# Giving out the last layer's result as one sequence of 32 blocks, with the next batch's messages between them

## The chip, the cores and the metric

The kernel runs on one core of one Trainium2 chip. The metric is device time in microseconds (us) of one execution; lower is better. A core has five engines that run side by side, each through its own instructions in order: TensorE (PE in the profile, its weight loads PEld), VectorE (DVE), ScalarE (ACT), GpSimd (POOL) and SyncE (SP), which here issues nearly all DMAs.

## The reference

Four layers work on `x` of shape 4 x 128 x 128 x 128 (batch, two spatial axes, channels), each as `x = x + layer(groupnorm(x))`: a deformable convolution, a scan of 1-D convolutions over rows, a message layer, and a triangle layer. The change touches only the code of the last two:

```
def _L2_conv_ref(inputs, Wself, Wm, Wk):
    message_m = sum(inputs, axis=2); message_k = sum(inputs, axis=1)
    return inputs @ Wself.T + (message_m @ Wm.T)[:, :, None, :] + (message_k @ Wk.T)[:, None, :, :]

def _L3_conv_ref(x, ...):
    xn = layer_norm(x, norm_g, norm_b)
    left  = (xn @ left_w  + left_b)  * sigmoid(xn @ lgate_w + lgate_b)
    right = (xn @ right_w + right_b) * sigmoid(xn @ rgate_w + rgate_b)
    out_gate = sigmoid(xn @ ogate_w + ogate_b)
    out = einsum('bkjd,bkid->bijd', left, right)
    out = layer_norm(out, onorm_g, onorm_b) * out_gate
    return out @ to_out_w + to_out_b
```

The group norm ahead of each layer has 32 groups of 4 channels. All data are 32-bit floats.

## The kernel before, in words

`tile_preact_convs` calls `deform_layer` (layer 0), `scan_layer` (layer 1) and `message_and_triangle` (layers 2 and 3) one after the other. The last one starts near 4116 us; it is the subject here. It goes through the four batches `b`. `X` (in on-chip memory, 128 x 128 x 128) holds a batch's x3, the input of the triangle layer; `L` (same size) the left factor, later the triangle's result; `R_0` and `R_1` hold a quarter of the right factor each, and between batches quarters of the input `x2T`. In DRAM lie `x3d` (x3, for the residual) and `gates` (the output gates). Sizes: a group is `JG` = 32 columns, a block `JB` = 4 columns, so a batch has 4 groups of 8 blocks; the projections are cut into `NQ` = 4 quarters of 32 hidden channels and go in blocks of `QB` = 8 columns.

For a batch, the stages are lists of closures that each emit a few instructions on several engines:

- `sums_of(b)`: `prelude` (group-norm factors and message vectors), 32 `rows` items (L1321 one matmul of 512 columns, L1327 four DVE operations that add the messages and write X, L1332 one ACT square that sums), and `close`, which stores all of X to `x3d` by four DMAs of 2 MB (L1343) and makes the scale `s3` and shift `t3` of layer 3's group norm. `fetch` (L1311) loads a quarter of `x2T` (2 MB) into `R`; two quarters are fetched near the last triangle, the other two from within `rows`.
- `turned(b, g)`: for each block of group g, scale X in place (ACT, L1398), transpose on PE (L1406), copy back (ACT, L1407), statistics on DVE (L1409); `close` computes the layer norm's factors (L1370 to L1381, with one square root on ACT).
- `spread(b, g)`: normalize (DVE, L1426), transpose back (L1435, L1436), gate matmul and sigmoid (L1441, L1445), and store the gate (L1446).
- `projected(b, q, ...)`: for quarter q, 16 blocks over the whole batch, each of 8 matmuls (16 in the profile, L1466), one sigmoid (ACT, L1470) and two products (DVE, L1472, into `L` and `R[q % 2]`).
- `triangle(b, q)`: 8 blocks of matmuls of R with L (L1484) and an ACT copy into L (L1488).
- `counted_out(b, g)`: DVE statistics of L (L1499) and the factors.
- `given(b, g)`: a software pipeline over the 8 blocks of group g. Step k loads the gate of block k+1 (L1514) and the x3 columns of block k (L1520), normalizes block k (ACT L1529, DVE L1534), turns block k-1 (PE transpose L1544, ACT L1546, POOL product with the gate L1547), and puts block k-2 (PE L1555 and L1559 add residual and output projection, DVE L1564 or ACT L1562 copies to `res`, SP stores it, L1565). So each group has 10 steps, of which the last two only drain.

The order on every engine, SP's DMA queue included, is the order in which closures run (`manual_schedule`). `weave` interleaves lists evenly by their lengths:

```
n = min((i for i in range(len(parts)) if done[i] < len(parts[i])),
        key=lambda i: (2 * done[i] + 1) / len(parts[i]))
```

A batch then goes: `turned(b, 0)` alone; for g = 0 to 4 a weave of `turned(b, g + 1)`, `spread(b, g)` and the quarter-0 projection of group g - 1 (the norm stage); for q = 1 to 3 a weave of `projected(b, q)` over the whole batch with `triangle(b, q - 1)`; `triangle(b, 3)`; then `counted_out(b, 0)` woven with the first half of `sums_of(b + 1)`; then the four `given(b, g)`, each woven with `counted_out(b, g + 1)`, the first also with the second half of `sums_of(b + 1)`.

Buffers that matter: `work` (two, shared by the square's output, the sigmoid and the product with the gate), `res` (two), gate and `x3cols` (three each), and three pools of two PSUM buffers: `ps_q` for message sums and projections, `ps_t` for transposes and triangle, `ps_g` for gates, output and small sums.

Of the kernel before, what the change touches and what calls it, by code (L numbers as in the profile page):

```python
# [9 lines left out]
F32 = mybir.dt.float32  # L10
I32 = mybir.dt.int32
BF16 = mybir.dt.bfloat16
AF = mybir.ActivationFunctionType
# [43 lines left out]
def make_consts(nc, pool):  # L57

    c = Consts()
    c.ident = pool.tile([P, P], F32, name="ident")  # L60
    make_identity(nc, c.ident)
    c.ones = pool.tile([P, P], F32, name="ones")
    nc.vector.memset(c.ones, 1.0)
    c.mean = pool.tile([P, P], F32, name="mean")
    nc.vector.memset(c.mean, 1.0 / P)

    c.center = pool.tile([P, P], F32, name="center")
    nc.vector.tensor_scalar(c.center, c.ident, -1.0 / P, None, ALU.add)

    c.gmean = pool.tile([P, P], F32, name="gmean")  # L70
    nc.vector.memset(c.gmean, 1.0 / GS)
    gview = c.gmean.rearrange("p (g r) -> p g r", r=GS)
    nc.gpsimd.affine_select(
        out=gview, in_=gview, pattern=[[-GS, NGN], [0, GS]], compare_op=ALU.is_ge,
        fill=0.0, base=0, channel_multiplier=1,
    )
    nc.gpsimd.affine_select(
        out=gview, in_=gview, pattern=[[GS, NGN], [0, GS]], compare_op=ALU.is_ge,
        fill=0.0, base=GS - 1, channel_multiplier=-1,
    )  # L80
    c.eps = pool.tile([P, 1], F32, name="eps")
    nc.vector.memset(c.eps, GN_EPS)
    return c
# [1094 lines left out]
def message_and_triangle(tc, c, x2T, x3d, gates, counted, w2, w3, out):  # L1178
# [10 lines left out]
    JB = 4  # L1189
    QB = 8  # L1190
    QC = 4 * DQ
    NW = NQ * QC
    with ExitStack() as ctx:
        wp = ctx.enter_context(tc.tile_pool(name="l3w", bufs=1))
# [80 lines left out]
        def prelude(b):  # L1275
# [6 lines left out]
            msg = one.tile([P, 2, S], F32, name="msg")  # L1282
            nc.vector.tensor_scalar(msg[:, 0], sum_w[:, b], s2, tsum, ALU.mult, ALU.add)
            nc.vector.tensor_scalar(msg[:, 1], sum_h[:, b], s2, tsum, ALU.mult, ALU.add)
            twide = one.tile([P, S], F32, name="twide")
            nc.vector.tensor_scalar(twide, c.ones, t2, None, ALU.mult)
            pm = small_ps([P, 2, S], "msg_ps")
            nc.tensor.matmul(pm[:, 0], lhsT=wm, rhs=msg[:, 0], start=True, stop=False)
# [24 lines left out]
        def sums_of(b):  # L1313

            todo = [lambda: prelude(b)]

            def rows(y0):
                ws, z, less, lessb, squares = got[b]
                at = y0 % DQ
                pz = ps_q.tile([P, JB, S], F32, name="self_ps", tag="ps_q")  # L1320
                nc.tensor.matmul(  # L1321
                    pz, lhsT=ws, rhs=R[y0 // DQ % 2][:, at : at + JB, :], start=True, stop=True
                )
                if at + JB == DQ and y0 + DQ < S:
                    fetch(b, y0 // DQ + 2)
                for i in range(JB):
                    nc.vector.scalar_tensor_tensor(  # L1327
                        X[:, :, y0 + i], pz[:, i], z[:, 0, y0 + i : y0 + i + 1], z[:, 1],
                        ALU.add, ALU.add,
                    )  # L1330
                junk = two.tile([P, S, JB], F32, name="work", tag="work")
                nc.scalar.activation(  # L1332
                    junk, X[:, :, y0 : y0 + JB], AF.Square, bias=lessb,
                    accum_out=squares[:, y0 // JB : y0 // JB + 1],
                )

            todo += [lambda y0=y0: rows(y0) for y0 in range(0, S, JB)]

            def close():
                _, _, less, lessb, squares = got[b]  # L1340
                for g in range(NG_J):
                    js = slice(g * JG, (g + 1) * JG)
                    nc.sync.dma_start(x3d[b, :, js, :], X[:, js, :])  # L1343
                e = one.tile([P, 1], F32, name="e3")
                nc.vector.tensor_reduce(e, squares, AX.X, ALU.add)
                pg = small_ps([P, 1], "mean_ps")
                nc.tensor.matmul(pg, lhsT=c.gmean, rhs=less, start=True, stop=True)
                lg = one.tile([P, 1], F32, name="lg3")
                nc.vector.tensor_copy(lg, pg)
                d = one.tile([P, 1], F32, name="d3")  # L1350
                nc.vector.tensor_tensor(d, less, lg, ALU.subtract)
                nc.vector.tensor_tensor(d, d, d, ALU.mult)
                nc.vector.scalar_tensor_tensor(d, e, 1.0 / (S * S), d, ALU.mult, ALU.add)
                pv = small_ps([P, 1], "var_ps")
                nc.tensor.matmul(pv, lhsT=c.gmean, rhs=d, start=True, stop=True)
                var = one.tile([P, 1], F32, name="var3")
                nc.vector.tensor_copy(var, pv)
                s3 = two.tile([P, 1], F32, name="s3")
                nc.scalar.activation(s3, var, AF.Sqrt, bias=c.eps)
                nc.vector.reciprocal(s3, s3)  # L1360
                t3 = two.tile([P, 1], F32, name="t3")
                nc.vector.scalar_tensor_tensor(t3, lg, outb, s3, ALU.subtract, ALU.mult)
                got[b] = (s3, t3)

            return todo + [close]

        def factors(stats, name):

# [21 lines left out]
        def turned(b, g):  # L1390
# [8 lines left out]

            def block(k):  # L1400
                j0 = g * JG + k * JB
                if (k + 1) * JB < JG:
                    scale(k + 1)
                pt = ps_t.tile([P, JB, S], F32, name="turn_ps", tag="ps_t")
# [98 lines left out]

            return [lambda k=k: block(k) for k in range(JG // JB)] + [close]

        def given(b, g):

            n = JG // JB
            pend = {}

            def load(k):
                j0 = g * JG + k * JB
                gt = three.tile([P, JB, S], F32, name="gate", tag="load")
                nc.sync.dma_start(gt, gates[b, :, j0 : j0 + JB, :])  # L1514
                pend[k] = (gt,)

            def load_x3(k):
                j0 = g * JG + k * JB
                xr = three.tile([P, JB, S], F32, name="x3cols")
                nc.sync.dma_start(xr, x3d[b, :, j0 : j0 + JB, :])  # L1520
                pend[k] += (xr,)

            def norm(k):
                mu, r, off = known["o", b, g]
                cen = normed[k % 2]
                for j in range(JB):
                    i = k * JB + j
                    if j % 2:
                        nc.scalar.activation(  # L1529
                            cen[:, j], L[:, :, g * JG + i], AF.Identity,  # L1530
                            bias=off[:, i : i + 1], scale=r[:, i : i + 1],
                        )
                    else:
                        nc.vector.tensor_scalar(  # L1534
                            cen[:, j], L[:, :, g * JG + i], mu[:, i : i + 1], r[:, i : i + 1],
                            ALU.subtract, ALU.mult,
                        )
                pend[k] += (cen,)
# [9 lines left out]
                pend[k] = (xr, a)  # L1548

            def put(k):  # L1550
                j0 = g * JG + k * JB
                xr, a = pend.pop(k)
                po = ps_g.tile([P, JB, P], F32, name="out_ps", tag="ps_g")
                for j in range(JB):
                    nc.tensor.matmul(  # L1555
# [1 line left out]
                        start=True, stop=False,  # L1557
                    )
                    nc.tensor.matmul(po[:, j], lhsT=a[:, j], rhs=outw, start=False, stop=True)  # L1559
                res = two.tile([P, JB, P], F32, name="res")  # L1560
                if k % 2:
                    nc.scalar.copy(res, po)  # L1562
                else:
                    nc.vector.tensor_copy(res, po)  # L1564
                nc.sync.dma_start(out[b, :, j0 : j0 + JB, :], res)  # L1565

            def step(k):
                if k == 0:
                    load(0)
                if k + 1 < n:  # L1570
                    load(k + 1)
                if k < n:
                    load_x3(k)
                    norm(k)
                if 1 <= k <= n:
                    turn(k - 1)
                if k >= 2:
                    put(k - 2)

            return [lambda k=k: step(k) for k in range(n + 2)]  # L1580

        def run(todo):
            for f in todo:
# [3 lines left out]
        ctx.enter_context(tc.manual_schedule(engines=order))  # L1587
        for i in range(2):
            fetch(0, i)
        run(sums_of(0))  # L1590
        for b in range(B):

            for t in normed:
                nc.vector.memset(t[:, :, 0:1], 1.0)
            run(turned(b, 0))
            for g in range(NG_J + 1):
                run(weave(
                    turned(b, g + 1) if g + 1 < NG_J else [],
                    spread(b, g) if g < NG_J else [],
                    projected(b, 0, (g - 1) * JG, g * JG) if g else [],  # L1600
                ))
            for q in range(1, NQ):
                run(weave(projected(b, q, 0, S), triangle(b, q - 1)))
            fetch(b + 1, NQ % 2)
            run(triangle(b, NQ - 1))
            fetch(b + 1, 1 - NQ % 2)

            ahead = sums_of(b + 1) if b + 1 < B else []
            half = len(ahead) // 2
            run(weave(counted_out(b, 0), ahead[:half]))  # L1610
            ahead = ahead[half:]
            for g in range(NG_J):
                run(weave(
                    counted_out(b, g + 1) if g + 1 < NG_J else [], given(b, g),
                    ahead if g == 0 else [],
                ))


@with_exitstack
# [69 lines left out]
```

## Time and profile before

| what | us |
|---|---|
| median of three runs (lowest, highest) | 5844.51 (5839.72, 5850.21) |
| the profiled execution | 5849.12 |
| its span in the profile | 5847.4 |
| PE busy in the span | 5267.0 (90%) |
| DVE | 3312.0 (57%) |
| ACT | 2790.1 (48%) |
| POOL | 782.5 (13%) |
| norm stage of batch 0, 4203.1 to 4317.0 | 113.9 (PE 98.3, ACT 81.9, DVE 70.5, clock 0.90) |
| projections and triangles of batch 0, 4317.0 to 4437.7 | 120.7 (PE 118.8, clock 1.00) |

How to read it: the span is the profile's time from first to last instruction. Busy time counts an engine's own instructions; PE's matmuls are pipelined and their ends are modelled, so their busy time overstates how full PE is. The granted clock is the share of full speed that TensorE was given in a window. In rows of instruction groups, the numbers after the first bar are the total busy time and the mean duration of one in ns, after the second bar the engine's idle time just before them and what ended it. "SPq" rows are DMA issues on SP's queue. The page cuts the span into 40 slices of 146 us: the last eleven or so are the part the change touches.

### The profile page before, as it was taken

How to read it: one execution, taken by the hardware profiler on the slowest of the kernel's cores; microseconds unless marked ns; L12 is line 12 of the kernel's file. 1: busy time of each engine (PE TensorE's matmuls, PEld its weight loads, DVE VectorE, ACT ScalarE, POOL GpSimd, SP SyncE). 2: the span in 40 equal slices, each digit the busy share in tenths (PEclk: the TensorE clock that was granted, in tenths of full speed). 3: DMA queues.
4: the chain of work that ended last, by engine and by line, in shares of the span. 5: the costliest groups of instructions: out<-in, count | busy, mean ns of one | idle time of the engine just before them, and what ended most of it. 6: DMA issues, size and time to landing. Idle time of an engine off the chain costs nothing. (4 is left out here: it accounts for less than half of the span.)

```text
span 5847.4 us, 112110 instructions
## 1 busy us (share of the span) xinstructions
PE 5267.0 (90%) x42401; PEld 4483.6 (77%) x42401; DVE 3312.0 (57%) x10356; ACT 2790.1 (48%) x5852; POOL 782.5 (13%) x674
## 2 busy tenths in 40 slices
PE   2899999999999999999999799999597697796796
PEld 1778888888888888888888699999375585584585
DVE  5544444554445544444333399999656556656656
ACT  1355554455554555545444233333454654644745
POOL 2021211011110111211000022222000200200102
PEclk9899999999999999999999899999799898898898
DMA  4555554555555555545433222332313513404414
GB/s 144 139 135 131 140 131 113 132 123 131 134 127 123 122 134 130 136 114 113 86 76 71 64 87 87 94 95 80 144 41 133 175 39 148 168 32 172 145 39 164
DMA packets 1130041, 671.44 MB, mean 115 GB/s; under 512 B 736205, under 2 KB 1002638, under 8 KB 1113110
## 3 DMA queue, kind: packets, MB, share of 16 engines
q1 hardware_dynamic: 1119346, 657.77, 42.4%
q8 instruction: 338, 5.54, 0.4%
q10 hardware_dynamic: 10148, 6.43, 0.4%
q14 instruction: 209, 1.71, 0.1%
HBM read 382.88 MB, written 281.11 MB: 114 GB/s over the span
## 5 line engine op out<-in xcount | busy, mean ns | idle before, releaser
L512 DVE TENSOR_TENSOR m<-ty,t_ps 120x390 f32<-120x390 f32 x1548 | 804.8, 557 | 1500.2 <-ACT ty L510 1499.0
L523 PEld LDWEIGHTS v_ps<-m,pixels 120*128 120x128 f32 x11352 | 1438.7, 194 | 86.3 <-issue 9.3
L523 PE MATMUL v_ps<-m,pixels 120*128 120x108 f32 (+1 forms) x11352 | 1464.7, 273 | 3.6 <-ACT v L533 3.5
L533 ACT COPY v<-v_ps 128x432 f32<-128x432 f32 x1376 | 719.7, 523 | 1271.8 <-PE v_ps L523 1269.0
L581 PE MATMUL conv_ps<-v,wdef 128*128 128x128 f32 (+2 forms) x5160 | 1303.2, 379 | 6.3 <-DVE x1c L554 5.8
L581 PEld LDWEIGHTS conv_ps<-v,wdef 128*128 128x128 f32 x5160 | 813.8, 192 | 256.0 <-issue 22.0
L510 ACT COPY ty<-t_ps 120x390 f32<-120x390 f32 x1560 | 688.3, 489 | 178.1 <-PE t_ps L500 170.7
L500 PE MATMUL t_ps<-places,spread 25*120 25x99 bf16 (+1 forms) x10836 | 520.0, 259 | 62.5 <-DVE m L512 38.9
L500 PEld LDWEIGHTS <-spread 25*120 25x120 bf16 x10896 | 339.0, 136 | 224.8 <-issue 123.2
L1466 PEld LDWEIGHTS proj_ps<-wcat,X 128*128 128x128 f32 x4096 | 475.7, 192 | 29.1 <-issue 29.1
L1466 PE MATMUL proj_ps<-wcat,X 128*128 128x128 f32 x4096 | 484.5, 275 | 0.5
L395 POOL TENSOR_TENSOR off<-off,koff 72x512 f32<-72x512 f32 x128 | 162.0, 1266 | 2299.8 <-DVE off L392 2221.8
L1547 POOL TENSOR_TENSOR work<-work,gate 128x512 f32<-128x512 f32 x128 | 166.1, 1302 | 1574.9 <-ACT work L1546 1440.7
L1071 ACT ACTIVATE rowT<-x1T_ps,t_x,s_x 128x128 f32<-128x128 f32 x512 | 192.7, 457 | 366.0 <-PE x1T_ps L1064 346.7
L1084 PE MATMUL m_ps<-carry,w 128*128 128x172 f32 x2286 | 361.3, 310 | 0.0
L1472 DVE TENSOR_TENSOR L<-proj_ps,work 128x256 f32<-128x256 f32 x256 | 155.1, 606 | 352.3 <-ACT work L1470 352.3
L1084 PEld LDWEIGHTS m_ps<-carry,w 128*128 128x128 f32 x2286 | 345.5, 188 | 0.0
L1151 POOL TENSOR_TENSOR sum_h<-sum_h,x2c 128x512 f32<-128x512 f32 x128 | 162.4, 1269 | 1163.4 <-DVE x2c L1148 1163.4
L1470 ACT ACTIVATE work<-proj_ps 128x512 f32<-128x512 f32 x256 | 152.8, 597 | 298.9 <-PE proj_ps L1466 298.9
L1559 PE MATMUL out_ps<-outw,work 128*128 128x128 f32 x1024 | 206.3, 304 | 43.5 <-POOL work L1547 43.2
L1555 PE MATMUL out_ps<-ident,x3cols 128*128 128x128 f32 x512 | 152.6, 298 | 95.4 <-DMA x3cols<-x3d 95.3
L1559 PEld LDWEIGHTS out_ps<-outw,work 128*128 128x128 f32 x1024 | 174.7, 214 | 57.0 <-POOL work L1547 56.2
(231 smaller groups left out, 6693.7 us busy)
## 6 DMA issues: line engine op xcount, KB each, us to landing
pixels<-tab SPq DMA_DIRECT2D x688, 123.8 KB
xin<-in_x_dram SPq DMA_DIRECT2D x56, 1024.0 KB
off<-parts SPq DMA_DIRECT2D x64, 891.0 KB
tab<-rows SPq DMA_DIRECT2D x384, 128.0 KB
places<-off SPq DMA_DIRECT2D x688, 55.7 KB
x<-x1c SPq DMA_DIRECT2D x32, 1024.0 KB
x1rows<-x SPq DMA_DIRECT2D x128, 256.0 KB
x2T<-x2c SPq DMA_DIRECT2D x128, 256.0 KB
```

The lines of the kernel that those rows point to most:

```text
L500: nc.tensor.matmul(to, lhsT=spread[p0 : p0 + KROWS, ph, :], rhs=mov, start=True, stop=True,)
L510: nc.scalar.copy(ty[:, 0:n], tp[0:LANES, 0, 0:n])
L512: nc.vector.tensor_tensor(m, ty[:, 0:n].rearrange("p (r c) -> p r c", c=PADW), tx, ALU.mult)
L523: nc.tensor.matmul(vp[:, h * n : h * n + rows * w].rearrange("p (k c) -> p k c", c=w), lhsT=pix[0:LANES, xb, :], rhs=m[:, :, RX * xb : RX ...
L533: nc.scalar.copy(v[:, :, c0 : c0 + 4 * RX].rearrange("p k (h c) -> p k h c", c=RX), vp[:, 0 : 4 * n].rearrange("p (h k c) -> p k h c", h=4 ...
L581: nc.tensor.matmul(pc[:, at : at + r1 - r0, :], lhsT=wdef[:, 3 * ky + kx, :], rhs=v[:, k0 + kx, r0:r1, kx : kx + S], start=m == 0, stop=m ...
L1071: nc.scalar.activation(rt[:, b, :], px[:, b, :], AF.Identity, bias=t, scale=s)
L1084: nc.tensor.matmul(to, lhsT=wgt, rhs=src[:, :, at : at + n], start=i == 0, stop=i + 1 == len(todo),)
L1151: nc.gpsimd.tensor_tensor(sum_h, sum_h, x2c[:, :, i], add)
L1466: nc.tensor.matmul(pp[:, j], lhsT=X[:, j0 + j, :], rhs=wcat[:, cols], start=True, stop=True)
L1547: nc.gpsimd.tensor_tensor(a, a, gt, ALU.mult)
L1559: nc.tensor.matmul(po[:, j], lhsT=a[:, j], rhs=outw, start=False, stop=True)
```

## The change

- `sums_of(b + 1)` is followed at once by `turned(b + 1, 0)`; of this list the first 6 items (`FIRST`: the prelude and 5 rows) are woven with `counted_out(b, 0)`, the other 40 with the giving out. For batch 0 both run alone as before.
- `given(b)` is one pipeline of 32 blocks (35 steps); each 8 steps are woven with the next group's `counted_out`. The store of a block's result is moved from the end of its put to the start of the next step; `res` has three buffers.
- x3 is stored by groups, as two DMAs of 1 MB each: group 0 when the sums end (`means`), group g + 1 from block 2 of `turned(b, g)`. The group-norm `close` is split into `means`, `variances` and `close`.
- In the norm stage, quarter 1 is projected beside quarter 0; `triangle(b, 0)` then runs alone, and the later projections start at quarter 2.
- The square's output has a buffer of its own (`junk`, one), shared with `twide`. The unused constant `center` goes.

```diff
-    c.center = pool.tile([P, P], F32, name="center")
-    nc.vector.tensor_scalar(c.center, c.ident, -1.0 / P, None, ALU.add)
...
+    FIRST = 6
...
-                junk = two.tile([P, S, JB], F32, name="work", tag="work")
+                junk = one.tile([P, S, JB], F32, name="junk", tag="junk")
...
-            def close():
+            def means():
                 _, _, less, lessb, squares = got[b]
-                for g in range(NG_J):
-                    js = slice(g * JG, (g + 1) * JG)
-                    nc.sync.dma_start(x3d[b, :, js, :], X[:, js, :])
+                kept_columns(b, 0)
...
-            return todo + [close]
+            return todo + [means, variances, close]
+
+        def kept_columns(b, g):
+
+            for h in range(2):
+                js = slice(g * JG + h * JG // 2, g * JG + (h + 1) * JG // 2)
+                nc.sync.dma_start(x3d[b, :, js, :], X[:, js, :])
...
             def block(k):
                 j0 = g * JG + k * JB
+                if k == 2 and g + 1 < NG_J:
+                    kept_columns(b, g + 1)
...
-        def given(b, g):
-
-            n = JG // JB
+        def given(b):
+
+            n = S // JB
...
-                res = two.tile([P, JB, P], F32, name="res")
+                res = three.tile([P, JB, P], F32, name="res")
...
-                nc.sync.dma_start(out[b, :, j0 : j0 + JB, :], res)
+                pend[k] = res
+
+            def store(k):
+                nc.sync.dma_start(out[b, :, k * JB : (k + 1) * JB, :], pend.pop(k))
 
             def step(k):
+                if 3 <= k:
+                    store(k - 3)
...
-                if k >= 2:
+                if 2 <= k <= n + 1:
                     put(k - 2)
 
-            return [lambda k=k: step(k) for k in range(n + 2)]
+            steps = [lambda k=k: step(k) for k in range(n + 3)]
+            todo = []
+            for g in range(NG_J):
+                now = steps[g * JG // JB : (g + 1) * JG // JB]
+                todo += weave(counted_out(b, g + 1) if g + 1 < NG_J else [], now)
+            return todo + steps[n:]
...
-        run(sums_of(0))
+        run(sums_of(0) + turned(0, 0))
         for b in range(B):
...
-            run(turned(b, 0))
             for g in range(NG_J + 1):
                 run(weave(
                     turned(b, g + 1) if g + 1 < NG_J else [],
                     spread(b, g) if g < NG_J else [],
                     projected(b, 0, (g - 1) * JG, g * JG) if g else [],
+                    projected(b, 1, (g - 1) * JG, g * JG) if g else [],
                 ))
-            for q in range(1, NQ):
+            run(triangle(b, 0))
+            for q in range(2, NQ):
                 run(weave(projected(b, q, 0, S), triangle(b, q - 1)))
...
-            ahead = sums_of(b + 1) if b + 1 < B else []
-            half = len(ahead) // 2
-            run(weave(counted_out(b, 0), ahead[:half]))
-            ahead = ahead[half:]
-            for g in range(NG_J):
-                run(weave(
-                    counted_out(b, g + 1) if g + 1 < NG_J else [], given(b, g),
-                    ahead if g == 0 else [],
-                ))
+            ahead = sums_of(b + 1) + turned(b + 1, 0) if b + 1 < B else []
+            run(weave(counted_out(b, 0), ahead[:FIRST]))
+            run(weave(given(b), ahead[FIRST:]))
```

More of the change, by code (lines that the diff above doesn't have):

```diff
@@ L1284, in prelude @@
             nc.vector.tensor_scalar(msg[:, 1], sum_h[:, b], s2, tsum, ALU.mult, ALU.add)
-            twide = one.tile([P, S], F32, name="twide")
+            twide = one.tile([P, S], F32, name="twide", tag="junk")
             nc.vector.tensor_scalar(twide, c.ones, t2, None, ALU.mult)
@@ L1337, in sums_of @@
             todo += [lambda y0=y0: rows(y0) for y0 in range(0, S, JB)]
-            def close():
+            part = {}
+            def means():
                 _, _, less, lessb, squares = got[b]
-                for g in range(NG_J):
-                    js = slice(g * JG, (g + 1) * JG)
-                    nc.sync.dma_start(x3d[b, :, js, :], X[:, js, :])
-                e = one.tile([P, 1], F32, name="e3")
+                kept_columns(b, 0)
+                e = part["e"] = one.tile([P, 1], F32, name="e3")
@@ L1345, in close, with variances @@
                 nc.vector.tensor_reduce(e, squares, AX.X, ALU.add)
-                pg = small_ps([P, 1], "mean_ps")
+                pg = part["pg"] = small_ps([P, 1], "mean_ps")
                 nc.tensor.matmul(pg, lhsT=c.gmean, rhs=less, start=True, stop=True)
-                lg = one.tile([P, 1], F32, name="lg3")
+                lg = part["lg"] = one.tile([P, 1], F32, name="lg3")
                 nc.vector.tensor_copy(lg, pg)
+            def variances():
+                _, _, less, lessb, squares = got[b]
@@ L1350, in close @@
                 d = one.tile([P, 1], F32, name="d3")
-                nc.vector.tensor_tensor(d, less, lg, ALU.subtract)
+                nc.vector.tensor_tensor(d, less, part["lg"], ALU.subtract)
                 nc.vector.tensor_tensor(d, d, d, ALU.mult)
-                nc.vector.scalar_tensor_tensor(d, e, 1.0 / (S * S), d, ALU.mult, ALU.add)
+                nc.vector.scalar_tensor_tensor(d, part["e"], 1.0 / (S * S), d, ALU.mult, ALU.add)
                 pv = small_ps([P, 1], "var_ps")
                 nc.tensor.matmul(pv, lhsT=c.gmean, rhs=d, start=True, stop=True)
-                var = one.tile([P, 1], F32, name="var3")
+                var = part["var"] = one.tile([P, 1], F32, name="var3")
@@ L1357, in close @@
                 nc.vector.tensor_copy(var, pv)
+            def close():
                 s3 = two.tile([P, 1], F32, name="s3")
-                nc.scalar.activation(s3, var, AF.Sqrt, bias=c.eps)
+                nc.scalar.activation(s3, part["var"], AF.Sqrt, bias=c.eps)
                 nc.vector.reciprocal(s3, s3)
                 t3 = two.tile([P, 1], F32, name="t3")
-                nc.vector.scalar_tensor_tensor(t3, lg, outb, s3, ALU.subtract, ALU.mult)
+                nc.vector.scalar_tensor_tensor(
+                    t3, part["lg"], outb, s3, ALU.subtract, ALU.mult
+                )
@@ L1504, in counted_out @@
             return [lambda k=k: block(k) for k in range(JG // JB)] + [close]
-        def given(b, g):
-            n = JG // JB
+        def given(b):
+            n = S // JB
             pend = {}
             def load(k):
-                j0 = g * JG + k * JB
                 gt = three.tile([P, JB, S], F32, name="gate", tag="load")
-                nc.sync.dma_start(gt, gates[b, :, j0 : j0 + JB, :])
+                nc.sync.dma_start(gt, gates[b, :, k * JB : (k + 1) * JB, :])
                 pend[k] = (gt,)
             def load_x3(k):
-                j0 = g * JG + k * JB
                 xr = three.tile([P, JB, S], F32, name="x3cols")
-                nc.sync.dma_start(xr, x3d[b, :, j0 : j0 + JB, :])
+                nc.sync.dma_start(xr, x3d[b, :, k * JB : (k + 1) * JB, :])
                 pend[k] += (xr,)
             def norm(k):
-                mu, r, off = known["o", b, g]
+                mu, r, off = known["o", b, k * JB // JG]
                 cen = normed[k % 2]
                 for j in range(JB):
-                    i = k * JB + j
+                    i = k * JB % JG + j
                     if j % 2:
                         nc.scalar.activation(
-                            cen[:, j], L[:, :, g * JG + i], AF.Identity,
+                            cen[:, j], L[:, :, k * JB + j], AF.Identity,
                             bias=off[:, i : i + 1], scale=r[:, i : i + 1],
@@ L1534, in norm @@
                         nc.vector.tensor_scalar(
-                            cen[:, j], L[:, :, g * JG + i], mu[:, i : i + 1], r[:, i : i + 1],
+                            cen[:, j], L[:, :, k * JB + j], mu[:, i : i + 1], r[:, i : i + 1],
                             ALU.subtract, ALU.mult,
@@ L1550, in put @@
             def put(k):
-                j0 = g * JG + k * JB
-                xr, a = pend.pop(k)
+                xr, a = pend[k]
                 po = ps_g.tile([P, JB, P], F32, name="out_ps", tag="ps_g")
```

## The prediction, made before the result was known

> **What bounds the kernel now.** I read the page first: TensorE's clock and busy digits, and DMA's, fall into a pattern of four in the last quarter of the span. The change touches only this part (the last layers, 4116 us to the end; the chain has its first step there at 4101.94 + 14.04). Then the busy time by windows, cut at the first and last instruction of each stage, here for the giving out of batch 0 with the messages of batch 1, the next batch's two stages, and the last batch.
>
> ```profile
> 4440.30:4471.50 31.20, 21.29 (x42) 7.44 (x42) 28.49 (x111) 12.14 (x31) 0.00 (x0) 0.89 0.29 119
> 4471.50:4525.00 53.50, 36.92 (x171) 23.38 (x170) 41.42 (x150) 33.38 (x73) 10.79 (x8) 0.88 0.53 192
> 4525.00:4545.00 20.00, 0.37 (x3) 0.29 (x2) 1.02 (x4) 1.76 (x3) 1.44 (x2) 0.50 0.98 394
> 4545.00:4620.90 75.90, 56.43 (x376) 49.53 (x375) 49.95 (x128) 43.03 (x76) 29.13 (x23) 0.88 0.70 229
> 4620.90:4634.30 13.40, 6.16 (x32) 3.94 (x32) 8.31 (x40) 10.74 (x19) 0.00 (x0) 0.79 0.06 22
> 4634.30:4749.90 115.60, 98.34 (x513) 67.75 (x513) 70.39 (x271) 81.22 (x135) 0.00 (x0) 0.89 0.19 73
> 4749.90:4870.90 121.00, 119.07 (x1055) 118.34 (x1056) 53.59 (x102) 48.57 (x82) 0.00 (x0) 1.00 0.05 19
> ...
> 5726.00:5737.00 11.00, 0.00 (x0) 0.00 (x0) 10.17 (x40) 1.97 (x3) 0.00 (x0) 0.58 0.00 0
> 5737.00:5844.00 107.00, 76.62 (x512) 65.24 (x512) 76.00 (x201) 65.90 (x115) 41.60 (x32) 0.87 0.67 220
> ```
>
> Columns: window and length, busy PE, weight loads, VectorE (DVE), ScalarE (ACT), POOL, granted clock, DMA share, GB/s. Only the projection stage (121 us) has a full engine: PE, 119 of 121. In the 31 us of statistics and messages DVE is full (28.5). In the third row nothing computes: DMA is 98% busy. In the rest no engine is above 80%. So I asked what ends the waits there. The chain of that stretch, in order of time, has
>
> ```profile
> 4525.85 18.82 DMA x3cols<-x3d
> ```
>
> right after the 8.4 MB store of x3 (4519.9 to 4523.2 on SP's queue): the load of x3 columns stands behind it. The timeline of SP's queue at the end of a group of 8 blocks, here in the last batch, shows the other stall:
>
> ```profile
> 5758.33 4.98 SPq L1565 DMA_DIRECT2D out_dram<-res  x3
> 5763.42 0.87 SPq L1514 DMA_DIRECT2D gate<-gates  x2
> 5764.38 0.39 SPq L1520 DMA_DIRECT2D x3cols<-x3d  x1
> ```
>
> SP waits with each store for its result, so the next group's first loads go out only after the old group has drained. In the timeline the starts of L1546 in that batch are 5739.4, 5741.1, 5745.2, 5748.3, 5750.1, 5753.8, 5755.5, 5758.6, and the next groups begin at 5765.2, 5792.5, 5819.3. Inside a group the four middle steps (3.2, 1.8, 3.7, 1.7) make 2.6 us each; a group takes 27.1. So 27.1 - 8 x 2.6 = 6.3 us go at each of three boundaries.
>
> **The change, part by part.** The first 4116 us are the same but for one VectorE instruction (c.center) at the start: 0.
>
> *x3 stored by groups.* The 20 us of idle, once in each of three batches (4525 to 4545, 4956 to 4980, 5385 to 5404), end. In place of one queue of 8.4 MB, 2.1 MB are stored before giving out reaches its last third, 2.1 MB some steps later, and 4.2 MB in the norm stage, where DMA is 19% busy: no cost there. Against this split speaks the Trainium skill (DMA: Bandwidth & Descriptors, section "Anatomy of one DMA"): a fixed 2 us or so for each DMA beside its bytes, stated for GpSimd's path. Eight stores of 1 MB in place of four of 2 MB would by this estimate cost 4 x 2 = 8 us a batch if they stood alone. The row above says otherwise: 394 GB/s moves 8.4 MB in 21 us, so queued stores hide their fixed parts. I take 0. But each 2.1 MB piece holds loads behind it for 2.1/394 = 5.3 us; so do the two quarters of R that were fetched before giving out began and now come inside it. A load is issued about two steps before its use, 5 to 8 us, of which its own landing takes up to 4.3 (the chain's piece for a gate issued at 5764.86). Cost between 0 and 5.3 for each of four pieces; I take 1, together 4 us a batch. If the cover is gone it is 21.
>
> *One sequence of 32 blocks.* Three boundaries x 6.3 = 19 us a batch vanish if the steps keep 2.6 us. SP's order inside a sequence is unchanged (the deferred store stands just ahead of the next loads, where it stood before); res with three buffers frees the waits on out stores, 4.2 us in all (releasers of out_ps). What is late next: the DMA. A block moves 3 x 0.262 = 0.79 MB; at 229 GB/s with a share of 0.70 the full rate for these pieces is 327 GB/s, so a step can't be under 2.4 us. In the last batch I take 2.75 (between 2.6 and 3.0): 31 steps = 85 us where L1546 now runs from 5739.4 to 5839.5 (100): 14 us saved, 7 to 19.
>
> *Messages and turned(b+1, 0) inside.* The 13.4 us of turned group 0 (4620.9 to 4634.3), alone on ACT now, move under giving out for b = 0 to 2. Rows are paid by DVE: four L1327 take 1.21 us, and the middle stage (16 rows, 10 steps, 53.5 us) gives 2.6 a step plus 1.2 a row plus 8 us of start, drain and end. New stage: opening 31.2 minus 11 rows x 1.1 = 19; first 22 steps with 27 rows 22 x 2.6 + 27 x 1.2 + 3 for the fill = 93; last 12 steps at 2.6 = 31, with 8 turned blocks at 1.0 (ACT 0.81 + 0.58, DVE 0.87, partly under the step's slack: 0 to 1.4), 8, and 6 for means, variances, close and the final factors; 4 of DMA. Sum 161. Before, from the message start to the first norm: 194.0 (4440.3 to 4634.3), 190.6, 191.5, mean 192. Saved 31 a batch, 93 for three. Check by DVE: 28.5 + 41.4 + 1.0 + 50.0 + 8.3 = 129 us busy, so 161 is 80% of DVE, as rows 1 and 2 together have (69.9 of 84.7).
>
> Batch 0's start: L1398 waits 3.7 us for the store of x3; with 1 MB ahead of it in place of 2 and the issue moved before the mean's chain, about 3 us less. junk has its own buffer: removes 1.3 us of waits on POOL, counted as 0.
>
> *Two projections in the norm.* Out of the PE-bound stage go 16 blocks of 16 matmuls, (36.0 - 7.6)/16 = 1.77 us each (36.0 between the projections' first matmuls, 7.6 the triangle's share by the chain): 28.4 us a batch. Into the norm stage go the same 16 blocks, each 1.8 us of PE, 0.60 of ACT (L1470) and 1.2 of DVE (L1472 twice).
>
> ```profile
> L1466 PE MATMUL proj_ps<-wcat,X 128*128 128x128 f32 x3936 | 464.8, 275 | 0.5
> ...
> L1472 DVE TENSOR_TENSOR L<-proj_ps,work 128x256 f32<-128x256 f32 x247 | 149.7, 606 | 337.9 <-ACT work L1470 337.9
> ...
> L1470 ACT ACTIVATE work<-proj_ps 128x512 f32<-128x512 f32 x246 | 146.9, 597 | 290.5 <-PE proj_ps L1466 290.5
> ```
>
> PE is busy 98 of 115.6 in the norm, which looks like little room, but is inflated: 275 ns is a matmul's latency, and 16 go by in 1.80 us, 112 ns each. Real occupancy at full clock is near 79 us. So there is room, yet the weave runs in order: ACT waits for each block (290 us in all before L1470). The nearest row: the group without projections takes 24.3 us (norm starts 4634.3, 4658.5; mean of four batches), those with four blocks 30.7, so a block costs 1.6 us net. A second block directly behind the first finds no head start left: 1.8 on PE. Exception: at a group's start PE sits idle 2.8 us for the first scale (4689.9 to 4692.7), and the second block falls there. Bounds for 16 blocks: 5 us (PE's room used) to 58 (PE, ACT, DVE in series, 3.6 each). I take 16 x 1.62 = 26: 2.5 us a batch saved, 10 in all. The clock: windows around each group start give 0.50 for 6.8 us, 1.00 between. The Trainium skill (TensorE: Matmul & The Clock Gate, "What's actually happening") has it that an idle window of about 3.4 us halves the clock and a busy one restores it; by that, filling the 2.8 us would free up to 3 x 3.4 us a batch, 40 in all. The row puts the half clock after the idle time at the boundary, part of which (scale behind the table load) stays, and the half-rate time is only partly on PE. I count nothing and keep it for the range. Triangle 0 alone: same 7.6 us of PE.
>
> **Sum.** 93 + 14 + 3 + 10 = 120. The profiled execution took 5849.1 us (span 5847.4 plus 1.7 around it), 4.6 above the median 5844.5 of three; 5849.1 - 120 = 5729, at the median 5724.5. Predicted 5725.
>
> **Rivals.** (1) DMA takes the place of the removed wait. For it: 33.6 MB in a stage of 161 us, and in its last third 12 x 2.4 + 10.6 = 39 of 45 us; prefetch is only two steps deep. Against: mean share about 0.6. If each of four pieces costs 5.3 in full and steps go at 2.9, the stage takes 17 + 34 x 0.3 = 27 us more, and the last batch saves 10: 120 - 81 - 4 = 35 left; half of that damage is likelier, 78 left: 5767. Chance 0.18.
> (2) The second projection hides well and the clock rises: the norm grows by 5 us a batch, 23 saved in place of 2.5: 82 more, 5642. For it: PE's room. Against: 1.6 us net for the first block. Chance 0.11.
> (3) Slower: the second projection stands in series on PE, ACT and DVE, half of the blocks at half clock: (3.6 + 5.4)/2 = 4.5 us a block, 64 x (4.5 - 1.77) = 175 us lost against 110 won elsewhere: 5910. It decides from 110/64 + 1.77 = 3.5 us a block on. The marginal 1.6 speaks against. Chance 0.04.
> The forecast itself has 0.67, with 5685 to 5765 from its bounds (stage +-9 a batch, last batch +-6, norm -15 to +10). Against the 0.2% (12 us) that a measurement of this kernel tells from no change: faster 0.95, same 0.02, slower 0.03. Range 5660 to 5792: it takes in (1) up to three quarters of its damage, and leaves out most of (2) and (3).
>
> **What would show it.** Right: no stretch of idle near a store of x3; L1546 at an even pitch across blocks 8, 16, 24; message start to first norm near 161; norm stage some 26 longer and the projections 28 shorter. Wrong: x3cols waits of 3 us and more after each big transfer (rival 1); a norm stage under 125 (2) or over 170 (3).

## The result, and the profile after

The changed kernel takes 5766.5 us (median of four, 5763.4 to 5773.3) against 5842.1 before (median of four): a ratio of 0.9868, with an interval of 0.9856 to 0.988. That is 76 us less; the prediction had 5725, 120 less, with a range that holds 5766. Its profiled span is 5763.2, 84 below the 5847.4 of before.

The windows of the changed kernel answer to those of before. The first row is the whole stretch from the message start of batch 3 (the last that has messages) to its first norm, with the opening, the giving out and the turned group 0; then the norm stage and the projections of batch 1; then the last batch's two pieces. (Batches count from 0.)

```profile
5247.10:5420.70 173.60, 125.29 (x620) 89.24 (x620) 121.95 (x427) 100.25 (x199) 40.62 (x32) 0.81 0.57 200
...
4608.00:4748.40 140.40, 125.56 (x801) 96.16 (x801) 88.29 (x308) 91.20 (x153) 0.00 (x0) 0.96 0.23 91
4748.40:4836.70 88.30, 86.48 (x767) 86.10 (x768) 34.73 (x66) 37.81 (x64) 0.00 (x0) 1.00 0.07 25
...
5651.50:5663.80 12.30, 0.03 (x1) 0.06 (x1) 11.87 (x46) 3.06 (x6) 0.00 (x0) 0.63 0.00 0
5663.80:5757.50 93.70, 72.22 (x501) 63.41 (x501) 76.15 (x195) 62.49 (x112) 41.24 (x32) 0.90 0.77 250
```

The first row is 173.6 us where 161 was forecast, and no engine in it is above 125.3 of 173.6. The norm's clock is 0.96 where it was 0.89. The instructions' start times, stage by stage:

| stretch | before | after | saved in all | forecast |
|---|---|---|---|---|
| message start to the next batch's first norm, three times | 194.0, 190.6, 191.5 | 175.2, 173.6, 173.6 | 54 | 93 |
| first norm to the last triangle, four times (mean) | 234.4 | 229.2 | 21 | 10 |
| last batch, end of triangle to its last L1546 (L1557 after) | 114.1 | 105.0 | 9 | 14 |
| start to the first norm of batch 0 | 4203.1 | 4199.2 | 4 | 3 |
| last triangle to message start, three times | 2.9 | 4.1 | -4 | 0 |

Both ends of a stretch are starts of instructions. The sum is 84, as the spans have it. The waits for transfers, first before, then after, both over all of the last layers from 4430 us on (columns: who waited for whom, us in total, times, longest):

```profile
POOL work L1547 <- DMA gate<-gates: 104.7, 9, 28.1
...
PE out_ps L1555 <- DMA x3cols<-x3d: 95.3, 33, 19.6
```

```profile
PE out_ps L1565 <- DMA x3cols<-x3d: 2.9, 6, 0.8
...
POOL work L1558 <- DMA gate<-gates: 0.8, 2, 0.4
```

What the change was to remove is gone: 95 us of waits for x3 columns became 3. At a group's end in the last batch SP's queue now goes straight on:

```profile
5683.70 0.34 SPq L1578 DMA_DIRECT2D out_dram<-res  x1
...
5684.13 0.38 SPq L1526 DMA_DIRECT2D gate<-gates  x1
...
5684.61 0.41 SPq L1531 DMA_DIRECT2D x3cols<-x3d  x1
```

So where did the rest of the expected gain go? Into the steps that carry message rows. The starts of L1557 in batch 1's giving out go from 4866.5 to 4960.5 over the first 18 steps, with 25 rows among them: 94.0 us. The forecast's rule, 2.6 a step and 1.2 a row, makes 46.8 + 30 = 76.8. With 2.6 a step, a row costs (94.0 - 46.8)/25 = 1.9 us. But the last batch, which has no rows, takes 53.6 us and not 46.8 for its first 18 steps (5664.9 to 5718.5); measured against these, a row costs (94.0 - 53.6)/25 = 1.6. Either way it is more than 1.2. The waits of that stretch (4863 to 4950) show where:

```profile
ACT junk L1330 <- DVE X L1325: 32.4, 21, 2.9
...
DVE X L1325 <- PE self_ps L1319: 16.5, 9, 3.8
PEld out_ps L1569 <- POOL work L1558: 14.6, 9, 1.9
```

and the timeline of one round of it, cut to what waits:

```profile
4907.51 1.25 DVE L1325 SCALAR_TENSOR_TENSOR X<-self_ps,z 128x128 f32<-128x128 f32 x4 [3.77 <-PE self_ps L1319]
...
4908.86 0.72 ACT L1330 ACTIVATE junk<-X,lessb 128x512 f32<-128x512 f32 x1 [2.19 <-DVE X L1325]
...
4911.10 0.72 ACT L1330 ACTIVATE junk<-X,lessb 128x512 f32<-128x512 f32 x1 [1.43 <-DVE X L1325]
...
4912.81 0.76 ACT L1557 ACTIVATE work<-gT_ps,ob,og 128x512 f32<-128x512 f32 x1
...
4913.65 1.27 POOL L1558 TENSOR_TENSOR work<-work,gate 128x512 f32<-128x512 f32 x1 [7.95 <-ACT work L1557]
...
4914.97 0.80 PE L1569 MATMUL out_ps<-outw,work 128*128 128x128 f32 x2 [1.57 <-POOL work L1558]
```

DVE stands for the row's matmul; ACT, in order, stands for DVE's row before it may square it, and behind the square waits the block's L1557; POOL waits for that, PE for POOL; and the next row's matmul is queued behind PE. It is a ring through four engines, each idle for a part of it. VectorE, the busiest of DVE, ACT and POOL, works for 71.34 of the 94 us:

```profile
4866.50:4960.50 94.00, 70.08 (x342) 48.01 (x340) 71.34 (x240) 55.10 (x116) 22.86 (x18) 0.86 0.58 196
```

My theory after the result: the row's own chain (PE, DVE, ACT) lies in order inside the block's ring (PE, ACT, POOL, PE), so a row costs more than DVE's 1.1 to 1.2. Rivals: DMA sets the step; DVE's throughput does; or the group boundaries still cost what they did, for another reason.

### The profile page after: what moved, and what is told of

Its sections match the earlier page's. It is cut to its first block, busy times and chain, and to the rows that moved or that the text cites. A ratio compares the mean times of both kernels' runs of the same rounds, so it can differ in the third digit from the quotient of the medians.

```text
span 5763.2 us, 112068 instructions
## 1 busy us (share of the span) xinstructions
PE 5261.4 (91%) x42401; PEld 4488.0 (78%) x42401; DVE 3294.4 (57%) x10355; ACT 2781.5 (48%) x5852; POOL 779.5 (14%) x674
## 5 line engine op out<-in xcount | busy, mean ns | idle before, releaser
L1569 PE MATMUL out_ps<-outw,work 128*128 128x128 f32 x1024 | 219.0, 316 | 69.6 <-POOL work L1558 69.6
L1325 DVE SCALAR_TENSOR_TENSOR X<-self_ps,z 128x128 f32<-128x128 f32 x512 | 152.4, 420 | 76.5 <-PE self_ps L1319 76.2
```

## The experiments

All medians are set against runs of the kernel before on the same chip, and ratios carry intervals of about +-0.0018 (10 us), so a difference of two kernels under some 13 to 15 us is not clear of noise. In us against the changed kernel I give the difference of ratios times 5842.

**One projection in the norm.** The line that projects quarter 1 in the norm is taken out, and the loop over quarters starts at 1 again:

```diff
-                    projected(b, 1, (g - 1) * JG, g * JG) if g else [],
...
-            run(triangle(b, 0))
-            for q in range(2, NQ):
+            for q in range(1, NQ):
```

> The changed kernel with only quarter 0 projected in the norm stage, quarters 1 to 3 woven with the triangles as before. By the traces the stages from the first norm to the last triangle fell from 234.4 to 229.2 us a batch. Theory (the second projection sits partly in idle time of PE and keeps its clock up): +21 us on the whole, 5788. Rival (that gain comes from elsewhere, such as the x3 stores in the norm stage or the start of a batch): within 5 us of the changed kernel's 5766.

Measured 5796.9, ratio 0.9906 (0.9888 to 0.9924): 22 us slower. First norm to last triangle is 234.0 in this kernel: the second projection is worth 5 us a batch, as the theory said. The message stages of this kernel are longer too (178.2 to 178.4 us from message start to first norm, for 173.6 to 175.2), which the theory has nothing for; why stays open.

**The whole store.** The sums' end stores all four groups; the later stores go.

```diff
-                kept_columns(b, 0)
+                for g in range(NG_J):
+                    kept_columns(b, g)
...
-                if k == 2 and g + 1 < NG_J:
-                    kept_columns(b, g + 1)
```

> The changed kernel, but x3 is stored whole (8.4 MB, eight DMAs) when the sums end, with everything else left. Theory (the idle of 20 us was the queue standing behind this store): +45 to +60 us, an idle stretch of 15 to 20 us in each of three batches. Rival (a longer sequence with loads under way would have hidden the store): under +15 us.

Measured 5818.4, ratio 0.9942 (0.9923 to 0.9961): 43 us slower, just under the theory's band. From the last triangle to the next norm it takes 192.4 to 195.4 us, against 177.7 to 179.3. The idle stretch is back, but with 7.9 to 8.6 us it is half of the 15 to 20 expected (first line, one of three). The waits for loads around it, one or two of each kind a batch, last up to 13.5 us, about the 14 that are lost a batch:

```profile
4575.00:4583.20 8.20, 0.00 (x0) 0.00 (x0) 0.00 (x0) 0.02 (x1) 0.00 (x0) 0.50 0.99 353
```

```profile
POOL work L1557 <- DMA gate<-gates: 39.5, 3, 13.5
...
PE out_ps L1564 <- DMA x3cols<-x3d: 37.6, 4, 12.6
```

**The grouped store alone.** The kernel before, with `kept_columns` called as in the change and nothing else:

```diff
-                for g in range(NG_J):
-                    js = slice(g * JG, (g + 1) * JG)
-                    nc.sync.dma_start(x3d[b, :, js, :], X[:, js, :])
+                kept_columns(b, 0)
...
+                if k == 2 and g + 1 < NG_J:
+                    kept_columns(b, g + 1)
```

> The kernel before with one part of the change alone: x3 stored by groups (group 0 at the end of the sums, group g + 1 from block 2 of the turning of group g). Theory (the idle of 20 us in three batches is the queue behind the whole store): -45 to -60 us against before, about 5790. Rival (each piece stalls the loads behind it by its 5.3 us, or holds the turning back): less than -25 us.

Measured 5799.8, ratio 0.9926 (0.991 to 0.9943): 43 us below before, a little short of the theory. Its waits in the giving out of one batch (4480 to 4620) have a part of the rival's stalls:

```profile
POOL work L1553 <- DMA gate<-gates: 23.0, 3, 11.4
...
PE out_ps L1561 <- DMA x3cols<-x3d: 13.4, 5, 5.9
```

Before, the same stretch had 7.0 and 7.9 us of these waits beside the one long wait of each behind the whole store. With groups one after the other, gates and columns still come late. In the changed kernel the same two waits are 0.8 and 2.9 in all.

**Skewed rows.** The row's matmul goes one row ahead, its square one row later; the work is the same. `rows` is split into `multiply` and `square`, and becomes

```diff
+                if y0 + JB < S:
+                    multiply(y0 + JB)
+                pz = ps.pop(y0)
                 for i in range(JB):
...
+                if y0:
+                    square(y0 - JB)
```

> The changed kernel with each message row spread over three items: its matmul is issued one row ahead, its square on ACT one row later; the same work. In the changed kernel's giving out a step with rows takes 5.2 us where I had forecast 4.15, ACT waits 32 us in 87 for X, DVE 16 us for the row's matmul. Theory (the rows' chain PE, DVE, ACT lies in order in the ring PE, ACT, POOL, PE of a block): about 1 us a step less, -15 us a batch, -45 in all, 5720. Rival (DMA or DVE sets the step): within 10 us of 5766.

Measured 5705.2, ratio 0.9753 (0.9734 to 0.9771): 67 us faster than the changed kernel. The 18 steps with 25 rows take 74.4 to 78.3 us: (76.2 - 46.8)/25 = 1.2 a row, what the forecast had assumed (0.9 against the 53.6 of steps without rows).

**Half of the skew each.** First only the square is later (`multiply(y0)` stays in its row), then only the matmul is ahead (`square(y0)` stays).

> Half of the skew: the changed kernel with each row's square on ACT issued one row later, its matmul where it was. In the changed kernel ACT waits 32 us in 87 for X just ahead of a square. If ACT's wait is the cause, nearly all of the skew's 60 us come: 5705 to 5725. If the wait of VectorE for the row's matmul is (16 us in 87): 5750 or more. If each lies in the ring: about half, 5735.

> The other half: the row's matmul issued one row ahead, its square where it was. If VectorE's wait for the matmul is the cause: 5705 to 5725. If ACT's wait for X is: 5750 or more. If each lies in the ring: about 5735.

Measured 5704.0 (ratio 0.9761, 0.9744 to 0.9777) and 5722.2 (0.9791, 0.9775 to 0.9807): 63 and 45 us faster than the changed kernel. Later squares alone give all of it. But the other half alone gives most of it too, which none of the three readings had: the two don't add. With the matmul ahead ACT still waits for DVE's rows nearly as long as in the changed kernel (first line, for 32.4), so that wait is not by itself the cost; slack at either place lets the ring turn faster. In the kernel with later squares ACT's wait (both 4853 to 4940, as long a stretch), its 18 steps with rows in batch 1, and the stage of batch 3 read

```profile
ACT junk L1328 <- DVE X L1343: 26.5, 16, 2.9
```

```profile
ACT junk L1328 <- DVE X L1341: 8.9, 7, 2.9
...
PEld out_ps L1584 <- POOL work L1573: 4.8, 6, 0.9
```

```profile
4845.00:4921.20 76.20, 61.13 (x339) 43.05 (x338) 74.36 (x237) 54.16 (x115) 23.18 (x18) 0.94 0.70 236
...
5206.50:5360.70 154.20, 117.04 (x620) 83.78 (x620) 126.91 (x427) 99.73 (x199) 41.06 (x32) 0.85 0.64 225
```

The same instructions as in the changed kernel's 173.6 take 154.2: DVE is 82% busy in place of 70%, DMA 64% in place of 57%, so neither had been at its limit. In the 18 steps with rows DVE is now: 74.36 of 76.20 us, 98% (95 to 98% in the three batches), where the changed kernel has 74 to 76%. With the whole skew it is 94 to 96%, with the matmul ahead 85 to 90%. With VectorE nearly full, the matmul's half has nothing left to win. The granted clock of these steps rose too (0.85 to 0.86 in the changed kernel, 0.89 to 1.00 in the three others); how much of the gain comes by the clock was not tried apart.

**All rows first.** `FIRST = 33` in place of 6.

> The changed kernel with FIRST = 33: all 32 message rows are woven with the statistics of group 0, ahead of giving out; only the closing sums and the turned group 0 stay inside it. Theory (a row costs 1.8 us or more inside the ring of a block, but only its VectorE time of 1.1 us where nothing else runs): opening stage near 50 us, giving out near 110, together about 12 us a batch less, -36 in all, 5730. Rival (VectorE or DMA sets the stage as a whole): 5766 or more.

Measured 5735.5, ratio 0.9809 (0.9793 to 0.9825): 34 us faster than the changed kernel, near the theory's 36. The opening takes 54.2 to 54.7 us, giving out 110 to 113. With 27 more rows the opening is 32.5 us longer than in the changed kernel: rows that stand outside the ring cost 1.2.

**Early factors.** The statistics of groups 1 to 3 are woven with 22 steps:

```diff
-            for g in range(NG_J):
-                now = steps[g * JG // JB : (g + 1) * JG // JB]
-                todo += weave(counted_out(b, g + 1) if g + 1 < NG_J else [], now)
-            return todo + steps[n:]
+            early = 22
+            for g in range(1, NG_J):
+                todo += counted_out(b, g)
+            return weave(todo, steps[:early]) + steps[early:]
```

> The changed kernel with the statistics of groups 1 to 3 woven with the first 22 steps in place of 24, so that a group's factors are ready 1 to 2 steps before its first block; the same work. In the changed kernel the last batch still loses about 3.3 us at each of three group boundaries (starts of the ACT step 5.5 and 4.8 apart where two steps take 5.2). Theory (the next group's factors, a chain over DVE, ACT and DVE, end just ahead of its first block): last batch -8 to -10 us, all four batches -20 to -35. Rival (DMA, busy over 0.9 of the time there, refills at the boundary and is the bound): last batch within 3 us.

Measured 5754.5, ratio 0.9841 (0.9822 to 0.9859): 16 us faster, but only 2 of it in the last batch (103.2 for 105.0), where the theory had 8 to 10: that is what the rival forecast. In the changed kernel a group there takes 23.9 us (starts of L1557 at 5686.5 and 5710.4, for one), where 8 x 2.6 would be 20.8: 3.1 are left at each boundary. With early factors that pause is gone from the boundary, but other steps grew (4.4, 5.0), so the whole hardly moved. VectorE's own work says why. These are, in the changed kernel's last batch, the eight steps just named, which have the next group's statistics beside them, and the last eight, which cross the last boundary and have none:

```profile
5686.50:5710.40 23.90, 17.90 (x128) 15.88 (x128) 21.96 (x62) 16.09 (x30) 10.41 (x8) 0.93 0.82 264
...
5734.40:5755.60 21.20, 15.78 (x115) 14.14 (x113) 12.29 (x18) 14.79 (x28) 10.32 (x8) 0.92 0.78 254
```

With the statistics, VectorE works for 22.0 us, which is more than 8 x 2.6; without them the steps take 21.2, only 0.4 over. Early factors shift the statistics, but leave as much of this work in the steps. No run took the statistics out alone. **Skewed rows with early factors** ask whether the two gains add:

> Skewed rows and early factors together, the same work as the changed kernel. If the two gains add (60 and 12 us): about 5693. If early factors only shift the statistics to steps that are full with rows: 5705 or more.

Measured 5710.1, ratio 0.9776 (0.976 to 0.9792): no better than the skew alone. VectorE is full in the steps with rows; and the waits for x3 columns, 4.5 us in all with the skew alone, are 24.5 here. Which of the two takes the gain was not tried apart.

**Fewer loads.** Early factors, with x3 columns loaded for three blocks of a batch only and used again for the other 29, so that it leaves out their residual.

```diff
-                xr = three.tile([P, JB, S], F32, name="x3cols")
-                nc.sync.dma_start(xr, x3d[b, :, k * JB : (k + 1) * JB, :])
-                pend[k] += (xr,)
+                if k < 3:
+                    xr = kept[k] = three.tile([P, JB, S], F32, name="x3cols")
+                    nc.sync.dma_start(xr, x3d[b, :, k * JB : (k + 1) * JB, :])
+                pend[k] += (kept[k % 3],)
```

> The kernel with early factors, but giving out loads the x3 columns of the first three blocks of a batch only and uses them again for all blocks (so the residual of the other blocks is left wrong); a third of giving out's traffic goes, no engine's work. Rival DMA (busy 0.9 of the time in the steady part, so it sets the 2.6 to 2.9 us a block): last batch at least -8 us against early factors, all four -25 or more. Theory (the ring through PE, ACT, POOL and DVE sets it): last batch within 3 us, the whole within 10 of 5754.

Measured 5747.5, ratio 0.9832 (0.9815 to 0.9848): 5 us below early factors, which the intervals don't tell from nothing; the last batch 101.3 for 103.2. The 18 steps with rows take 93.1 to 96.5 us, as in the kernel it is cut from (93.4 to 96.5). A third of the traffic is worth next to nothing: DMA isn't the bound, in this kernel. With the skew it was not tried.

**Late put.** Skewed rows, with `put(k - 3)` and `load_x3(k - 1)` in step k, three `work` and two `res` buffers.

> The kernel with skewed rows, and the put of a block (residual, output projection) one step later, with its x3 load one step later too, three buffers for the product and two for the result; the same work. Theory (PE waits for POOL's product of the block, 12 to 15 us in 87, and all behind it on PE waits too): -3 to -10 us a batch against skewed rows' 5705, about 5680. Rival (only the message rows were out of place in the ring): within 6 us of 5705.

Measured 5724.9, ratio 0.9798 (0.9782 to 0.9814): 26 us slower than skewed rows, against both expectations. The last batch gained (101.1 for 104.9), the three stages with messages lost (164.0 to 164.6 from triangle to norm, for 157.2 to 157.9). Its trace, from 4430 us on, has waits for DMA that skewed rows hardly have (4.5 us for x3 columns, 1.5 for stores of results):

```profile
PE out_ps L1584 <- DMA x3cols<-x3d: 22.7, 18, 4.3
...
DVE res L1593 <- DMA out_dram<-res: 9.2, 3, 3.6
```

The edit also moves a load and takes a result buffer, which fits them; the parts of the edit were not tried apart.

The version to keep is the one with later squares (or the whole skew): about 5705 us, ratio 0.976 to the kernel before and 63 to 67 us below the changed one.

## Why the prediction was right, and where a term was off

- *x3 by groups*: the mechanism was right, and no idle stretch is left. But it is worth 14 us a batch, not the 19 to 24 that the windows showed idle: 43 us are saved by it alone, and 43 lost when it alone is taken back. In the changed kernel the pieces cost less than the 4 us a batch I charged: all waits for x3 columns and gates are below 4 us in total. Rival 1 is out as the cause; fewer loads shows it once more.
- *One sequence*: "three boundaries x 6.3 = 19 us a batch vanish" was mis-sized. In the last batch 3.2 of each went and 3.1 stayed, so it saved 9 where I had 14. I had taken 2.6 from four middle steps of a group, but eight steps with statistics beside them have 22.0 us of VectorE work in their 23.9; the last eight, without, take 21.2. So most of what stayed is VectorE's work, and not a pause of the boundary.
- *Messages inside*: this is the failed term. "2.6 a step plus 1.2 a row" came out 17 us a batch too low in the 18 steps, more than the whole shortfall of 13 in that stage (174 for 161); the steps without rows gave some back. By the last batch's steps, 7 of the 17 are the steps' own (53.6 for 46.8) and 10 the rows' (1.6 for 1.2). The sum took VectorE's time as the price of a row, which holds only where VectorE is full; in the changed kernel it is 76% busy there and waits in the ring. I had read the 1.2 from a stage in which 8 us of "start, drain and end" took up the remainder; with nothing set aside, the same stage gives (53.5 - 26)/16 = 1.7 a row. My check by DVE's share (80%; the two rows that it leans on have 69.9 of 84.7, 83%) could not tell, because it assumed the share, and the changed kernel runs DVE at 70%. The price 1.2 is reached once the square has slack, so the engines allow it, and the order withheld it.
- *Two projections in the norm*: right in sign and small; 5.2 a batch for 2.5. A group with eight blocks takes 36.0 us (35.3 to 37.6), for 30.7 with four: 1.3 a block, below the 1.62 I took. From the first norm to the first triangle it takes 140.8 us on the mean for 119.2, and the rest 88.7 for 115.5: 22 longer and 27 shorter, for a forecast of 26 and 28. The granted clock of the norm stage rose, in batch 1 from 0.89 to 0.96. Here is one group start of that batch before (two more like it), and the two stretches at half clock after a group start in the changed kernel:

```profile
4693.50:4700.30 6.80, 6.25 (x22) 4.19 (x21) 4.46 (x18) 4.97 (x10) 0.00 (x0) 0.50 0.05 19
```

```profile
4671.50:4675.00 3.50, 3.28 (x10) 2.10 (x11) 3.50 (x17) 2.32 (x4) 0.00 (x0) 0.51 0.00 0
4709.10:4712.50 3.40, 3.40 (x12) 2.37 (x10) 0.95 (x4) 1.78 (x3) 0.00 (x0) 0.50 0.20 77
```

The Trainium skill (TensorE: Matmul & The Clock Gate, "What's actually happening") has it that an idle window of about 3.4 us halves the clock and a busy one restores it; the stretches of 6.8 and 3.4 us fit two and one of these windows. So the clock, which I put at nothing, did change. By the mean clocks of the four norm stages (0.91 before, 0.96 after) the time at half clock fell from about 21 to 11 us a batch, an estimate that takes the clock as either 1 or 0.5. The prediction's upper estimate of 40 us was not reached; how much of the 21 is clock and how much is hidden work was not tried apart. Rival 2 is out (the norm grew by 22 and not by 5), and so is rival 3, with no block near 3.5 us.
- *The sum*: 54 + 21 + 9 + 4 - 4 = 84 on the spans, for 120. The shortfall of 36 is 39 in the message stages, 5 in the last batch and 4 ahead of the messages, less 11 in the norm and 1 at the start. That the time came so near has luck in it: the norm's 11 more, in part by a term put at nothing, cover part of the rows' 39 less. The measured 5766.5 lies just above the 5685 to 5765 that the forecast itself had, and on the 5767 that rival 1 had as likelier; the waits, not the time, tell the two apart. The 4 us ahead of the messages are not explained.

## What to carry to other kernels

When work is woven into another pipeline whose engines run in order, price an item by the chain it puts in that ring, not by its busiest engine; give a hand-over between engines an item of slack (issue ahead, consume later), and try that before moving work about. Here no engine was busy for more than 72% of the stage, and 63 us lay in the order alone. Then look again at the steps themselves: once the order is mended, an engine may be full there (VectorE, 98%), and only less work on it can help. A stall that a window shows as idle is an upper bound: here 19 to 24 us a batch were worth 14. Taking a third of the traffic away tells at little cost whether DMA is the bound, for the kernel in which it is tried.

## What the runs showed that I had not expected

Breaking the ring at one of two places gave 45 or 63 us, and both together 67: later squares alone already fill VectorE in the steps with rows. And the whole store cost 14 us a batch either way, where I had expected its 20 us of idle. Put back into the changed kernel, it holds the loads up for 13 us only. Taken out of the kernel before, it takes the long waits with it, but others for gates and columns grow (7.0 and 7.9 us in one batch to 23.0 and 13.4); these fell under 4 us in all only with one sequence.
